# A cross-attention and FFN kernel: another prologue, the order of two small products, and where VectorE's spare work is put

## The chip, the cores and the metric

The kernel runs on one core of a Trainium2 chip. The metric is the device time of one execution in microseconds (us); the figure for a kernel is the median of its runs. One more execution was recorded by the profiler, and its rows are what the text below reads. The engines are TensorE (PE in the rows; PEld is its weight load), VectorE (DVE), ScalarE (ACT), GpSimd (POOL) and SyncE (SP, which here only issues transfers).

## What is computed

Sixteen samples `x` of 256 channels by 512 positions, all fp32. A layer norm over the positions, cross attention over channels-as-heads, a residual, another layer norm, and a feed-forward part whose weights are gathered from a table of 16 values:

```python
q = Wq @ norm(x) + bq; k = Wk @ ctx + bk; v = Wv @ ctx + bv      # per sample, 256x512
dot = einsum('bhdt,bhds->bhts', q, k) / sqrt(16)                 # 16 heads of 16 channels
mask = target_mask[..., :, None] * source_mask[..., None, :]
amap = softmax(mask * dot - (1 - mask) * 1e6, axis=-1) * mask
x = x + einsum('bhts,bhds->bhdt', amap, v)
n = norm(x)                                                     # rows of 512
gate, up = n @ lut[gate_idx].T, n @ lut[up_idx].T                # 512 -> 1376
x = x + (silu(gate) * up) @ lut[down_idx].T                      # 1376 -> 512
```

## The kernel before

The whole program is scheduled by hand: the order in which the Python code records instructions is the order on each engine.

**Attention.** `NK = 32` pairs of a sample and a channel half (k), each split into two units (u = 2k + e) of four heads, each unit into `NCH = 4` steps of 128 positions: 256 steps. Step s calls `scores(s + 7, s)`. For step s + 7 it makes the scores once (`pa`, L487) and VectorE reduces them to negated maxima (L503); for step s it makes the turned scores (`pb`, L495), which ScalarE exponentiates (L507). A padding row of the operands carries the maxima: `turn_max(u)` turns them by a small product (`pmx`, L512), VectorE copies them (`mx`, L514), and a transfer issued by POOL writes them into row 17 of each head of `qps` (L515). Another padding row carries the mask. `apply_v` (L529) multiplies with the values, `project` and `project_v` (both through L413) make q, k and v for later pairs. `pmx`, `pb`, and all of these projections share one pool of four PSUM buffers (`ps_b`).

Between the steps stand two dictionaries: `lumps[s]` holds PE work to be recorded in step s behind its scores, `after[s]` the rest. In 60 of the 64 units `turn_max` and a `project_v` fall into the same step, and before, `turn_max` is recorded first.

**The prologue.** Steps -7 to -1 only make scores and maxima. Ahead of them the first pair's tiles are made by `first_tile` (weights padded to the layout with gaps by `pad`, bias and mask added by VectorE at L371): the first unit's tiles ahead of step -7, the second unit's in steps -5 and -4. `warm` transposes the identity to keep PE at work while transfers land. `mbk` and `mb0` are the first sample's mask on all partitions, loaded with a broadcast; two small transfers patch rows of `mbk` (L380, L381).

**Lookups.** The gathered weights are built by VectorE from bit planes of the indices (`look_up`, L146 to L161). They are slotted between attention steps by a budget in ns:

```python
credit += 1930 + lasting[s] - taken[s] - (2590 if sa is not None else -500)
credit = min(credit, 1500.0)
while credit > 0:
    ns, op = next(queue, (0, None)); op(); credit -= ns
```

At step 229 (`turns - 3`) whatever is left of the `early` queue is recorded at once, and the first load of the `late` queue (`idx_r`) is issued.

**The FFN.** `gate_up(0..3, 0)`, then 84 units (p, o) of seven products each, a Strassen-like scheme: p is a pair of blocks of 512 columns, o a slice of 128 of the 1376 rows. The combined weights come from `combine_w` (L830), the combined inputs from `combine_x` (L839 to L842). The rest of the lookups and `combine_w` form one queue, `todo`; `fill(ns)` adds ns to a budget (capped at 3000) and records operations until it is spent. Units with p < 2 and o of 5 or 8 need weights that `todo` makes, so ahead of them the queue is drawn until they are recorded (`while o not in ready`). `turn_blocks` puts norm, turning and `combine_x` of later blocks into hooks of the units. Each unit calls its three hooks at three places.

Of the kernel before, what the change touches and what calls it, by code (L numbers as in the profile page):

```python
# [19 lines left out]
def kernel(  # L20
# [34 lines left out]
    nc = tc.nc  # L55
# [163 lines left out]
    with ExitStack() as att:  # L219
# [29 lines left out]
        def times(row, n):  # L249
            return row.rearrange("p (o t) -> p o t", o=1).to_broadcast([1, n, T])  # L250
# [45 lines left out]
        xn0 = p2.tile([P, NCC, T], F32, tag="xn", name="xn_0")  # L296
        mb0 = p2.tile([P, T], F32, tag="mb", name="mb_0")
        inp[0] = (cx0, xn0, mb0)
        for o in range(NCC):
            nc.sync.dma_start(xn0[:, o, :], x[0, o * P : (o + 1) * P, :])  # L300
        nc.scalar.dma_start(wk, wkT.rearrange("(o p) n -> p o n", p=P))
        nc.scalar.dma_start(cx0, src[0].rearrange("(o p) t -> p o t", p=P))
        nc.sync.dma_start(mk16, mask[:, 0, :])
        nc.sync.dma_start(mb0, mask[0, 0].partition_broadcast(P))

        w0 = pp.tile([P, 4, NCC, P], F32, tag="pt", name="w0")
        nc.gpsimd.memset(w0, 0.0)
        nc.gpsimd.memset(ones, 1.0)


        brow = pp.tile([P, P], F32, tag="pt", name="brow")
        nc.vector.memset(brow, 0.0)
        nc.vector.memset(brow[0:64, 16:P:32], NEG / QK)
        for i in range(2):
            nc.vector.memset(brow[64:P, 16 + i : P : 32], 1.0)

        mbk = pp.tile([P, T], F32, tag="pt", name="mbk")
        nc.sync.dma_start(mbk, mask[0, 0].partition_broadcast(P))
        nc.sync.dma_start(wq, wqT.rearrange("(o p) n -> p o n", p=P))
        for i, w in enumerate((bq, bk)):  # L320
            for e in range(2):
                at = 64 * i + 32 * e
                nc.gpsimd.dma_start(
                    brow[at : at + 1].rearrange("o (j e d) -> o j e d", e=2, d=D)[:, :, 0],
                    w[0:P].rearrange("(o j e d) -> o j e d", o=1, e=2, d=D)[:, :, e],
                )
# [6 lines left out]
        nc.scalar.dma_start(wv, wvT.rearrange("(o p) n -> p o n", p=P))  # L333
        nc.scalar.dma_start(bvb, bv.partition_broadcast(P))
        nc.scalar.dma_start(lut_b, lut.partition_broadcast(P))
        zeros = rpool.tile([P, T], F32, tag="rb", name="zeros", bufs=1)
        nc.gpsimd.memset(zeros, 0.0)

        def fill_rows():
            for i in (1, 0):  # L340
# [11 lines left out]
        def pad(i, e):  # L352
            w = (wk, wq)[i]
            to = w0[:, 2 * i + e].rearrange("p o (j r) -> p o j r", r=32)[:, :, :, 0:16]
            of = w[:, :, 0:P].rearrange("p o (j e d) -> p o j e d", e=2, d=D)[:, :, :, e]
            if i == 0:
                nc.vector.tensor_copy(to, of)
            else:
                nc.vector.tensor_scalar(to, of, QK, None, ALU.mult)

        def first_tile(which, e):
# [22 lines left out]
        pad(0, 0)  # L384
        rstd1_of(0, 1)
        norm1(0, nc.vector)
        pad(1, 0)
        pc = ps_b.tile([P, 512], F32, tag="b", name="pbrow")
        nc.tensor.transpose(pc[:, :P], brow, ident)
# [3 lines left out]
        first_tile("k", 0)  # L393
        first_tile("q", 0)
# [199 lines left out]

        lumps[-7].append(lambda: project(1, "k"))
        lumps[-6].append(lambda: project(1, "q"))
        after[-7].append(lambda: (pad(0, 1), pad(1, 1)))
        lumps[-5].append(lambda: first_tile("k", 1))
        lumps[-4].append(lambda: first_tile("q", 1))
# [66 lines left out]
        after[-4].append(lambda: set_ones(1))  # L666
# [85 lines left out]
        for s in range(min(min(after), min(lumps)), NSTEP + 2):  # L752
            sa = s + AHEAD if 0 <= s + AHEAD < NSTEP else None
            sb = s if 0 <= s < NSTEP else None
            if sa is not None or sb is not None:
                scores(sa, sb)
            for fn in lumps.pop(s, ()):
                fn()
            for fn in after.pop(s, ()):
                fn()  # L760
            if s >= 0:
                if s == turns - 3:
                    for _, op in early:
                        op()
                    load_rest()
                queue = early if s < turns - 3 else late
                credit += 1930 + lasting[s] - taken[s] - (2590 if sa is not None else -500)
                credit = min(credit, 1500.0)
                if s == NSTEP - 6:
                    closing.append(s)  # L770
                while credit > 0:
                    ns, op = next(queue, (0, None))
                    if op is None:
                        break
                    op()
                    credit -= ns
# [18 lines left out]
    with ExitStack() as ffn:  # L795
# [181 lines left out]
        def turn_blocks(n, at):  # L977

            k = 4 * n

            def step(i):
                if i:
                    turn2(k + i - 1)
                if i < 8:
                    norm2(k + i)
                    room[0] -= 550
                if i + 3 < 8:
                    load_x2(k + i + 3)
                if i == 8:
                    for _ in combine_x(n // 2):  # L990
                        room[0] -= 1230

            for i in range(3):
                hooks[at - 1, 2].append(lambda i=i: load_x2(k + i))
            for i in range(9):
                hooks[at + i // 3, i % 3].append(lambda i=i: step(i))
# [240 lines left out]
```

## Time and profile before

| what | us |
|---|---|
| median of 3 runs | 1821.81 (1821.67 to 1823.17) |
| profiled execution, its time | 1821.44 |
| profiled execution, its span | 1819.7 |
| TensorE busy | 1796.0 (99%) |
| VectorE busy | 1459.0 (80%) |
| ScalarE busy | 799.5 (44%) |
| GpSimd busy | 491.5 (27%) |
| first product of step -7 | 16.50 |
| first product of step 0 | 40.78 |

In the rows, the first number is the start from the beginning of the span, the second the duration, then engine, line, operation, output<-inputs, shape, and count; in brackets the idle time of that engine ahead of it and what ended it. In rows for a stretch each engine has its busy time and count, then the clock that TensorE was granted (1.00 is full), the share of the transfer engines in use, and GB/s.

### The profile page before, as it was taken

Reading aid. Unit: us, or ns where it says so; the run is one execution under the profiler, and the core shown is the slowest. Engines: PE = TensorE matmul, PEld = TensorE weight load, DVE = VectorE, ACT = ScalarE, POOL = GpSimd, SP = SyncE. Lnnn points to the kernel's source line nnn. Section 1 sums busy time; section 2 is a strip of 40 time slices with the busy share of each in tenths; the row PEclk is TensorE's granted clock in tenths of the full one; section 3 lists DMA queues with packets and bytes.
Section 4 is the critical chain, followed back from the end, with each engine's and each line's share of the span. In section 5 each row is a group of like instructions: output and inputs, shape, how many; then the busy total and the mean of one; then the engine's idle time right before and its main releaser. Section 6 shows DMA issues by size and latency. Waiting matters only on the chain.

```text
span 1819.7 us, 28550 instructions
## 1 busy us (share of the span) xinstructions
PE 1796.0 (99%) x10914; PEld 812.4 (45%) x10914; DVE 1459.0 (80%) x2030; ACT 799.5 (44%) x1523; POOL 491.5 (27%) x467
## 2 busy tenths in 40 slices
PE   8999999999999999999999999999999999999999
PEld 4333333333333333333234444444444444588887
DVE  6898988889898889898886799998888995353352
ACT  1777777777777777777676111112121111000000
POOL 4333343434333433433322122222222222000000
PEclk9999999999999999999999999999999999999999
DMA  6445534333433344444242211223231311533541
GB/s 187 129 143 149 149 115 129 121 114 96 127 114 125 92 128 137 148 121 141 87 120 75 69 58 55 74 81 106 68 104 42 116 51 44 182 132 126 176 132 58
DMA packets 118825, 201.07 MB, mean 111 GB/s; under 512 B 21781, under 2 KB 23961, under 8 KB 118689
## 3 DMA queue, kind: packets, MB, share of 16 engines
q1 hardware_dynamic: 114416, 196.21, 34.1%
q0 software_dynamic: 3168, 1.86, 0.5%
q8 instruction: 86, 1.41, 0.3%
q10 hardware_dynamic: 1104, 1.19, 0.2%
q14 instruction: 51, 0.41, 0.1%
HBM read 135.83 MB, written 58.10 MB: 107 GB/s over the span
## 4 chain that ended last, share of the span: by engine, by line
PE 92%; DVE 4%; DMA 1%; issue 0%; ACT 0%; SPq 0%; POOL 0%; ACTq 0%; DVEq 0%; POOLq 0%
PE p L934 27%; PE pa L487 15%; PE pv L529 12%; PE pb L495 11%; PE q L1140 11%; PE pv L413 3%; PE pq L413 3%; PE pk L413 3%; PE po L1121 2%; DVE nm L503 2%; PE q L1145 1%; PE pgu L914 1%; PE pmx L512 1%; PE pt L215 1%; DMA x2t<-x 1%; DVE chosen L161 0%
## 5 line engine op out<-in xcount | busy, mean ns | idle before, releaser
L503 DVE TENSOR_REDUCE nm<-pa 128x2 f32<-128x1024 f32 x512 | 603.3, 1220 | 103.8 <-PE pb L495 97.5
L507 ACT ACTIVATE pt<-pb 128x512 f32<-128x512 f32 x1024 | 530.0, 603 | 108.8 <-PE pb L495 107.7
L487 PE MATMUL pa<-kp,qp 32*128 32x512 f32 x2048 | 515.0, 616 | 9.5 <-DVE nm L503 6.9
L495 PE MATMUL pb<-qp,kp 32*128 32x512 f32 x2048 | 514.9, 617 | 0.0
L487 PEld LDWEIGHTS pa<-kp,qp 32*128 32x128 f32 x2048 | 179.5, 184 | 208.7 <-DVE nm L503 163.1
L529 PE MATMUL pv<-pt,va 128*32 128x512 f32 x2048 | 246.2, 598 | 0.0
L495 PEld LDWEIGHTS pb<-qp,kp 32*128 32x128 f32 x2048 | 203.4, 183 | 83.5 <-issue 52.4
L934 PE MATMUL p<-xe,wu 128*128 128x512 f32 (+1 forms) x336 | 158.1, 593 | 1.0 <-DVE w L938 1.0
L934 PE MATMUL p<-xT,sw 128*128 128x512 f32 (+1 forms) x336 | 157.9, 592 | 0.0
L934 PE MATMUL p<-xT,wg 128*128 128x512 f32 (+1 forms) x336 | 157.9, 592 | 0.0
L961 POOL TENSOR_TENSOR ha<-ha,sg 128x512 f32<-128x512 f32 (+1 forms) x42 | 60.4, 1438 | 344.3 <-DVE ha L938 326.0
L966 ACT ACTIVATE w<-w 128x512 f32<-128x512 f32 (+1 forms) x42 | 26.5, 630 | 241.4 <-DVE w L938 241.4
L529 PEld LDWEIGHTS pv<-pt,va 128*32 128x32 f32 x2048 | 53.4, 109 | 173.1 <-ACT pt L507 97.1
L515 POOL DMA_DIRECT2D qp<-mx x64 | 37.8, 591 | 313.1 <-DVE mx L514 290.4
L1156 ACT COPY q<-q 128x256 f32<-128x256 f32 x14 | 5.2, 372 | 254.4 <-PE q L1140 254.4
L534 ACT COPY us<-pv 128x512 f32<-128x512 f32 x128 | 74.9, 585 | 91.7 <-PE pv L529 91.0
L934 PEld LDWEIGHTS p<-xe,wu 128*128 128x128 f32 (+1 forms) x336 | 62.8, 187 | 83.0 <-issue 71.3
L934 PEld LDWEIGHTS p<-xT,wg 128*128 128x128 f32 (+1 forms) x336 | 62.7, 187 | 79.2 <-issue 75.4
L934 PEld LDWEIGHTS p<-xT,sw 128*128 128x128 f32 (+1 forms) x336 | 62.1, 187 | 75.4 <-issue 73.9
L948 ACT ACTIVATE sg<-sg 128x512 f32<-128x512 f32 (+1 forms) x42 | 26.5, 631 | 152.4 <-DVE sg L938 152.4
L541 POOL TENSOR_TENSOR us<-us,us 128x512 f32<-128x512 f32 x64 | 82.3, 1286 | 16.5 <-ACT us L534 16.5
L429 POOL TENSOR_TENSOR natk<-natk,mb 128x512 f32<-128x512 f32 x31 | 40.0, 1289 | 157.7 <-ACT natk L426 152.0
(205 smaller groups left out, 2375.1 us busy)
## 6 DMA issues: line engine op xcount, KB each, us to landing
x2t<-x SPq DMA_DIRECT2D x96, 256.0 KB
h<-h SPq DMA_DIRECT2D x7, 2560.0 KB
kp<-kd SPq DMA_DIRECT2D x62, 256.0 KB
qp<-qd SPq DMA_DIRECT2D x62, 256.0 KB
h<-ha SPq DMA_DIRECT2D x38, 256.0 KB
h<-hb SPq DMA_DIRECT2D x38, 256.0 KB
rb<-rd SPq DMA_DIRECT2D x32, 256.0 KB
xr<-in_x_dram SPq DMA_DIRECT2D x32, 256.0 KB
```

The lines of the kernel that those rows point to most:

```text
L413: nc.tensor.matmul(ps[32 * j : 32 * j + 32], weights(o, slice(first + 32 * j, first + 32 * j + 32)), moving(o), start=(o == 0), stop=(o == ...
L429: nc.gpsimd.tensor_tensor(t, t, mb, ALU.mult)
L487: nc.tensor.matmul(pa[:, jj, :], qps[ua % 4][at, ca * P : (ca + 1) * P], kps[ua % 4][at, :], start=True, stop=True,)
L495: nc.tensor.matmul(pb, kps[ub % 4][at, cb * P : (cb + 1) * P], qps[ub % 4][at, :], start=True, stop=True,)
L503: nc.vector.tensor_reduce(nms[ua][:, 2 * half : 2 * half + 2, ca], pa, AX.X, ALU.max, negate=True)
L507: nc.scalar.activation(pts[sb][:, j, :], pb, AF.Exp)
L529: nc.tensor.matmul(ps[32 * j : 32 * j + 32, :], va[:, at : at + 32], pt[:, j, :], start=(i == 0), stop=(i == 1),)
L534: nc.scalar.copy(us[u, half], ps)
L541: nc.gpsimd.tensor_tensor(a, a, b, ALU.add)
L934: nc.tensor.matmul(ps, a[:, h, at], b[:, h, :], start=h == 0, stop=h == 1)
L961: nc.gpsimd.tensor_tensor(ha, ha, sg, ALU.mult)
L1140: nc.tensor.matmul(ps, a[:, o, first_t], b[:, o, :], start=o == 0, stop=o == HO - 1 and not more,)
```

## The change

Six edits:

1. The prologue. VectorE's clearing of small tiles and the tiny transfers come first: two copies of the first mask row into `msrc`, and the bias entries into `brow`, the latter now issued by ScalarE's queue instead of POOL's. All large loads go to SP. `mbk` and `mb0` are no longer loaded with a broadcast; a product with a selection matrix `sel` spreads the mask rows (`pm`) and ScalarE copies the result. The warm-up has 16 and 24 transposes instead of 60. ScalarE does the padding for the second unit. All four first tiles are made ahead of step -7. `project(2, "k")` and `(2, "q")` move from steps -1 and 0 to -2 and -1; the first `project_v` go from steps -3 to -1 to steps -5 and -4; the loads of wv, bv and the table move to SP behind step -8; the filling of padding rows and the next loads from behind step -8 to behind -7.
2. `turn_max` is recorded behind `project_v` where both are in one step.
3. The credit is charged 2565 instead of 2590 ns per step.
4. `turn_blocks` starts one hook earlier.
5. `fill(6500)` is new ahead of `gate_up(0, 0)`; `fill(6000)` and `fill(3000)` around `gate_up(3, 0)` become one `fill(2500)`.
6. `combine_x(1)` is recorded operation by operation in hooks of the first unit (one in each of the first two, two in the third), each with `fill(-1230)`.

```diff
+        msrc = xpool.tile([P, T], F32, tag="xT", name="msrc")
+        sel = xpool.tile([P, 2, P], F32, tag="xT", name="sel")
+        nc.vector.memset(msrc, 0.0)
+        nc.vector.memset(brow, 0.0)
+        for i in range(2):
+            nc.sync.dma_start(msrc[32 * i : 32 * i + 1], mask[0, 0:1, :])
...
+                nc.scalar.dma_start(
+                    brow[at : at + 1].rearrange("o (j e d) -> o j e d", e=2, d=D)[:, :, 0],
...
-        nc.scalar.dma_start(wk, wkT.rearrange("(o p) n -> p o n", p=P))
-        nc.scalar.dma_start(cx0, src[0].rearrange("(o p) t -> p o t", p=P))
+        nc.sync.dma_start(wk, wkT.rearrange("(o p) n -> p o n", p=P))
+        nc.sync.dma_start(cx0, src[0].rearrange("(o p) t -> p o t", p=P))
+        nc.sync.dma_start(wq, wqT.rearrange("(o p) n -> p o n", p=P))
         nc.sync.dma_start(mk16, mask[:, 0, :])
-        nc.sync.dma_start(mb0, mask[0, 0].partition_broadcast(P))
...
-        nc.sync.dma_start(mbk, mask[0, 0].partition_broadcast(P))
-        nc.sync.dma_start(wq, wqT.rearrange("(o p) n -> p o n", p=P))
...
+            for o in range(NCC):
+                if e:
+                    nc.scalar.activation(to[:, o], of[:, o], AF.Copy, scale=QK if i else 1.0)
...
-        warm(60)
-        nc.vector.tensor_scalar(mk16, mk16, -1.0, None, ALU.add)
-        nc.sync.dma_start(mbk[16:P:32, :], times(mk16[0:1], 4))
-        nc.sync.dma_start(mbk[17:P:32, :], ones[0:4])
+        warm(16)
+        nc.vector.tensor_scalar(msrc[32:33], msrc[32:33], -1.0, None, ALU.add)
+        pm = ps_a.tile([P, 2, 512], F32, tag="a", name="pm")
+        for i, to in enumerate((mbk, mb0)):
+            nc.tensor.matmul(pm[:, i, :], sel[0:96, i, :], msrc[0:96], start=True, stop=True)
+            nc.scalar.copy(to, pm[:, i, :])
+        pc = ps_b.tile([P, 512], F32, tag="b", name="pbrow")
+        nc.tensor.transpose(pc[:, :P], brow, ident)
+        warm(24)
...
+        pad(0, 1)
+        pad(1, 1)
+        for e in range(2):
+            first_tile("k", e)
+            first_tile("q", e)
...
-        lumps[-1].append(lambda: project(2, "k"))
-        lumps[0].append(lambda: project(2, "q"))
+        lumps[-2].append(lambda: project(2, "k"))
+        lumps[-1].append(lambda: project(2, "q"))
...
-        for u in range(NU):
-            lumps[4 * u - 3].append(lambda u=u: turn_max(u))
-        lumps[-3].append(lambda: project_v(0, 0))
-        lumps[-2] += [lambda: project_v(0, 1), lambda: project_v(1, 0)]
-        lumps[-1].append(lambda: project_v(1, 1))
+        lumps[-5] += [lambda: project_v(0, 0), lambda: project_v(0, 1)]
+        lumps[-4] += [lambda: project_v(1, 0), lambda: project_v(1, 1)]
...
                 lumps[8 * k - 15 + 4 * i].append(lambda k=k, i=i: project_v(k, i))
                 after[8 * k - 13 + 4 * i].append(lambda k=k, i=i: mask_v(k, i))
+        for u in range(NU):
+            lumps[4 * u - 3].append(lambda u=u: turn_max(u))
...
-        after[-8] += [fill_rows, lambda: (load_xs(2), load_xs(3), load_b(1), load_wide(0))]
+        after[-8].append(load_v)
+        after[-7] += [fill_rows, lambda: (load_xs(2), load_xs(3), load_b(1), load_wide(0))]
...
-                credit += 1930 + lasting[s] - taken[s] - (2590 if sa is not None else -500)
+                credit += 1930 + lasting[s] - taken[s] - (2565 if sa is not None else -500)
...
-        turn_blocks(4, order.index((1, 8)))
-        turn_blocks(6, order.index((2, 5)))
+        turn_blocks(4, 3 * order.index((1, 8)) - 1)
+        turn_blocks(6, 3 * order.index((2, 5)) - 1)
...
+        fill(6500)
         gate_up(0, 0)
...
-        fill(6000)
+        fill(2500)
         gate_up(3, 0)
-        for _ in combine_x(1):
-            pass
-        fill(3000)
+        second = combine_x(1)
+        for i in range(4):
+            hooks[0, min(i, 2)].append(lambda: (next(second, None), fill(-1230)))
```

More of the change, by code (lines that the diff above doesn't have):

```diff
@@ L298 @@
         inp[0] = (cx0, xn0, mb0)
+        msrc = xpool.tile([P, T], F32, tag="xT", name="msrc")
+        sel = xpool.tile([P, 2, P], F32, tag="xT", name="sel")
+        brow = pp.tile([P, P], F32, tag="pt", name="brow")
+        nc.vector.memset(msrc, 0.0)
+        nc.vector.memset(brow, 0.0)
+        for i in range(2):
+            nc.sync.dma_start(msrc[32 * i : 32 * i + 1], mask[0, 0:1, :])
+        nc.vector.memset(brow[0:64, 16:P:32], NEG / QK)
+        for i in range(2):
+            nc.vector.memset(brow[64:P, 16 + i : P : 32], 1.0)
+        for i, w in enumerate((bk, bq)):
+            for e in range(2):
+                at = 64 * (1 - i) + 32 * e
+                nc.scalar.dma_start(
+                    brow[at : at + 1].rearrange("o (j e d) -> o j e d", e=2, d=D)[:, :, 0],
+                    w[0:P].rearrange("(o j e d) -> o j e d", o=1, e=2, d=D)[:, :, e],
+                )
         for o in range(NCC):
             nc.sync.dma_start(xn0[:, o, :], x[0, o * P : (o + 1) * P, :])
-        nc.scalar.dma_start(wk, wkT.rearrange("(o p) n -> p o n", p=P))
-        nc.scalar.dma_start(cx0, src[0].rearrange("(o p) t -> p o t", p=P))
+        nc.sync.dma_start(wk, wkT.rearrange("(o p) n -> p o n", p=P))
+        nc.sync.dma_start(cx0, src[0].rearrange("(o p) t -> p o t", p=P))
+        nc.sync.dma_start(wq, wqT.rearrange("(o p) n -> p o n", p=P))
         nc.sync.dma_start(mk16, mask[:, 0, :])
-        nc.sync.dma_start(mb0, mask[0, 0].partition_broadcast(P))
+        nc.vector.memset(msrc[64:65], 1.0)
+        nc.vector.memset(sel, 0.0)
+        nc.vector.memset(sel[0:1], 1.0)
+        for i in range(2):
+            nc.vector.memset(sel[0:1, 0, 16 + i : P : 32], 0.0)
+            nc.vector.memset(sel[32 + 32 * i : 33 + 32 * i, 0, 16 + i : P : 32], 1.0)
         w0 = pp.tile([P, 4, NCC, P], F32, tag="pt", name="w0")
@@ L308 @@
         nc.gpsimd.memset(ones, 1.0)
[L311 to L315, printed above, removed]
-        mbk = pp.tile([P, T], F32, tag="pt", name="mbk")
-        nc.sync.dma_start(mbk, mask[0, 0].partition_broadcast(P))
-        nc.sync.dma_start(wq, wqT.rearrange("(o p) n -> p o n", p=P))
[L320 to L326, printed above, removed]
+        mbk = pp.tile([P, T], F32, tag="pt", name="mbk")
         n = B * NCH
@@ L332, with load_v @@
         nc.gpsimd.dma_start(mq16, mask[:, 0, :])
-        nc.scalar.dma_start(wv, wvT.rearrange("(o p) n -> p o n", p=P))
-        nc.scalar.dma_start(bvb, bv.partition_broadcast(P))
-        nc.scalar.dma_start(lut_b, lut.partition_broadcast(P))
         zeros = rpool.tile([P, T], F32, tag="rb", name="zeros", bufs=1)
         nc.gpsimd.memset(zeros, 0.0)
+        def load_v():
+            nc.sync.dma_start(wv, wvT.rearrange("(o p) n -> p o n", p=P))
+            nc.sync.dma_start(bvb, bv.partition_broadcast(P))
+            nc.sync.dma_start(lut_b, lut.partition_broadcast(P))
         def fill_rows():
@@ L355, in pad @@
             of = w[:, :, 0:P].rearrange("p o (j e d) -> p o j e d", e=2, d=D)[:, :, :, e]
-            if i == 0:
+            for o in range(NCC):
+                if e:
+                    nc.scalar.activation(to[:, o], of[:, o], AF.Copy, scale=QK if i else 1.0)
+            if not e and i == 0:
                 nc.vector.tensor_copy(to, of)
-            else:
+            elif not e:
                 nc.vector.tensor_scalar(to, of, QK, None, ALU.mult)
@@ L376, in warm @@
                 nc.tensor.transpose(ps[:, :P], ident, ident)
-        warm(60)
-        nc.vector.tensor_scalar(mk16, mk16, -1.0, None, ALU.add)
-        nc.sync.dma_start(mbk[16:P:32, :], times(mk16[0:1], 4))
-        nc.sync.dma_start(mbk[17:P:32, :], ones[0:4])
+        warm(16)
[7 more added lines that the diff above has]
+        warm(24)
         for o in range(NCC):
             row_stats(p2, mv1[:, o, :], xn0[:, o, :], f"a0_{o}")
[L384 to L389, printed above, removed]
         bcol = pp.tile([P, P], F32, tag="pt", name="bcol")
@@ L392 @@
         nc.vector.tensor_scalar(bcol[:, 0:64], pc[:, 0:64], QK, None, ALU.mult)
-        first_tile("k", 0)
-        first_tile("q", 0)
+        rstd1_of(0, 1)
+        pad(0, 0)
+        norm1(0, nc.vector)
+        pad(1, 0)
+        pad(0, 1)
+        pad(1, 1)
+        for e in range(2):
+            first_tile("k", e)
+            first_tile("q", e)
+        nc.vector.tensor_scalar(mk16, mk16, -1.0, None, ALU.add)
         pc = ps_b.tile([P, 512], F32, tag="b", name="pcols")
@@ L596 @@
         lumps[-6].append(lambda: project(1, "q"))
-        after[-7].append(lambda: (pad(0, 1), pad(1, 1)))
-        lumps[-5].append(lambda: first_tile("k", 1))
-        lumps[-4].append(lambda: first_tile("q", 1))
         after[-6].append(lambda: send(1, "k"))
@@ L663 @@
             spread_out(stats_at[NCC * hi - 1] + 1, rstd1_of(lo, hi, newton_rstd))
-        after[-8] += [fill_rows, lambda: (load_xs(2), load_xs(3), load_b(1), load_wide(0))]
+        after[-8].append(load_v)
+        after[-7] += [fill_rows, lambda: (load_xs(2), load_xs(3), load_b(1), load_wide(0))]
         after[-7].append(lambda: set_ones(0))
-        after[-4].append(lambda: set_ones(1))
+        after[-6].append(lambda: set_ones(1))
         after[-2].append(lambda: norm1(1, nc.gpsimd))
@@ L993, in turn_blocks @@
             for i in range(3):
-                hooks[at - 1, 2].append(lambda i=i: load_x2(k + i))
+                hooks[divmod(at - 1, 3)].append(lambda i=i: load_x2(k + i))
             for i in range(9):
-                hooks[at + i // 3, i % 3].append(lambda i=i: step(i))
-        turn_blocks(4, order.index((1, 8)))
-        turn_blocks(6, order.index((2, 5)))
+                hooks[divmod(at + i, 3)].append(lambda i=i: step(i))
+        turn_blocks(4, 3 * order.index((1, 8)) - 1)
+        turn_blocks(6, 3 * order.index((2, 5)))
         for i in range(8):
```

## The prediction

> **What bounds the kernel now.** I read the page first: busy shares, then the chain that ended last.
>
> ```profile
> span 1819.7 us, 28550 instructions
> PE 1796.0 (99%) x10914; PEld 812.4 (45%) x10914; DVE 1459.0 (80%) x2030; ACT 799.5 (44%) x1523; POOL 491.5 (27%) x467
> ...
> PE 92%; DVE 4%; DMA 1%; issue 0%; ACT 0%; SPq 0%; POOL 0%; ACTq 0%; DVEq 0%; POOLq 0%
> ```
>
> TensorE is busy for 99% and carries 92% of the chain. No arithmetic of weight leaves it here, so the change can only win or lose in the places where TensorE waits. The table by stretches finds them (busy time of PE, PEld, DVE, ACT, POOL, then clock, DMA share, GB/s):
>
> ```profile
> 10.00:20.00 10.00, 7.48 (x40) 2.73 (x38) 5.82 (x13) 0.44 (x1) 2.58 (x5) 1.00 0.89 271
> 40.00:50.00 10.00, 8.41 (x86) 3.23 (x82) 7.75 (x9) 8.81 (x17) 4.24 (x5) 1.00 0.29 67
> ...
> 200.00:400.00 200.00, 199.02 (x1758) 69.37 (x1754) 178.71 (x216) 147.08 (x286) 79.23 (x76) 1.00 0.38 117
> ...
> 897.00:903.00 6.00, 1.97 (x20) 0.34 (x12) 5.93 (x6) 0.78 (x2) 1.08 (x1) 1.00 0.17 50
> 903.00:907.00 4.00, 4.00 (x24) 1.01 (x24) 3.60 (x9) 2.17 (x4) 0.00 (x0) 0.57 0.13 29
> ...
> 1190.00:1206.00 16.00, 16.00 (x39) 7.13 (x38) 15.83 (x29) 1.76 (x4) 3.68 (x3) 1.00 0.18 66
> ```
>
> TensorE loses time in the prologue and at 897, where the granted clock then falls to 0.57. Between 1190 and 1206 it loses none, but VectorE is full (15.83 of 16). Last, the timeline at these places, and one project_v unit:
>
> ```profile
> 15.04 0.75 DVE L371 SCALAR_TENSOR_TENSOR kp<-pk_first,bcol,mbk 128x512 f32<-128x512 f32 x1 [2.29 <-DMA mbk<-mrows]
> ...
> 17.68 2.36 DVE L503 TENSOR_REDUCE nm<-pa 128x2 f32<-128x1024 f32 x2 [0.58 <-PE pa L487]
> ```
> ```profile
> 41.36 1.28 ACT L507 ACT_TABLE_LOAD   x1
> 42.65 2.07 ACT L507 ACTIVATE pt<-pb 128x512 f32<-128x512 f32 x4
> ...
> 402.78 2.06 ACT L507 ACTIVATE pt<-pb 128x512 f32<-128x512 f32 x4 [0.42 <-PE pb L495]
> ```
> ```profile
> 403.51 0.41 PE L512 MATMUL pmx<-ident,nm 128*32 128x128 f32 x2
> 403.92 1.07 PE L413 MATMUL pv<-wv,ctx 128*32 128x256 f32 x16
> ...
> 901.97 0.69 PE L487 MATMUL pa<-kp,qp 32*128 32x512 f32 x1 [4.03 <-DVE nm L503]
> ```
> ```profile
> 894.82 1.17 DVE L157 TENSOR_SCALAR chosen<-chosen,lut_x,lut_b 128x688 int32<-128x688 int32 x2
> 896.02 3.83 DVE L161 COPY_PREDICATED chosen<-chosen,chosen 128x688 int32<-128x688 int32 x2
> 899.88 0.92 DVE L161 COPY_PREDICATED wg<-idx,chosen 128x688 int32<-128x688 int32 x1
> 900.70 2.34 DVE L503 TENSOR_REDUCE nm<-pa 128x2 f32<-128x1024 f32 x2
> ```
>
> **Part by part.** The sums are against the profiled execution (1821.44 us), which lies 0.37 below the median of the runs shown.
>
> *Prologue, +2.0.* Before, the first pa starts at 16.50 and its reduction at 17.68, held by the mask patch of mbk (15.04). After, a longer chain replaces it: msrc lands (estimate 4.3: issued about 1.3, then 3.0, as x1 took, whose landing let mbk be issued at 4.18), one VectorE operation, product pm0 (0.9 at the half clock of the start), ScalarE copy 0.6, pm1, copy 0.6, and then a second ACT_TABLE_LOAD: Copy now runs before the square root, so the load at 5.10 no longer hides under the loads. 1.28 + 0.30 + VectorE's 0.33, pad 0.21, norm1 1.08 and pad 0.23 bring the first product tiles to about 11.2; wq, issued once a tiny transfer has landed, comes at much the same time. Four first tiles at 1.72 (such groups start 1.71 to 1.78 apart) end at 18.1, so pa is 1.6 later; VectorE still owes qp1 (0.75) and two 0.42 operations, so the first reduction is about 2.5 later. Later, the two first tiles of steps -5 and -4 are gone from PE (2 x 1.72 = -3.4). Project(2,q) moves from step 0 into step -1, where it meets norm1(1): statistics (1.5 after the reduction of step -2), root, two small operations and POOL's 1.51 end 4.0 after that reduction, while PE is free 1.1 after it: +2.9. Sum 2.5 - 3.4 + 2.9 = +2.0; SP's and ACT's queues issue earlier or idle. POOL's six fills of padding rows (3.7 of issuing) stand behind natk and still land before the fetch at step -2; load_v on SP comes before step -7. Bounds: 0, if the q wait overlaps what ScalarE's exp table load (1.28) holds up in step 0 anyway; +4.5, if msrc or wq lands late.
>
> Here a rule speaks against the change: the Trainium skill, "ScalarE: Activation LUTs", What ACT_TABLE_LOAD costs, puts a switch at 1283 ns of load and about 1380 ns of drain, 2.66 us. The row at 41.36 shows 1.28, with the exp at its heels at 42.65, and the copy ahead ended at 41.34: no drain. By the row the sum stays; by the page it is 1.4 worse. I take the row.
>
> *project_v ahead of turn_max, -4.2.* In 60 units PE runs pmx in 0.41 for about 0.2 of work, since project_v then waits for the PSUM buffer that the second exp frees. Swapped, project_v takes the first exp's buffer and pmx the second's: at most 0.2 x 60 = 12. But the step after needs the fourth exp's buffer for its last pb: exps end at 404.84, and the step could start only slightly before its 404.92. I take 0.07 x 60 = 4.2 and keep +1 to -12. The copy of the maxima follows the reductions (ended 405.19) as before; its transfer has three steps to land.
>
> *credit 2590 to 2565, -3.3.* 25 ns in each of 229 steps lets 5.7 us of lookups start earlier, so the five operations at 894.82-900.7 are done by step 225. In the built order only two operations of the late set remain in step 229, and the first waits for idx_r, issued at 893.48 and landing, by an estimate from its packets, at 898.5. The reductions then start near 899.2 instead of 900.70, PE idles about 2.7 instead of 4.03. Steps start at 893.63, 901.97 and 907.66 where such steps take 3.78: 4.56 and 1.91 are lost, of which 1.4 and 1.9 return. Bounds -6 (idx_r early) and -1. Steady steps have 1.0 or more of VectorE slack, which covers 25 ns; without that cover the price would be 5.7.
>
> *combine_x(1) spread over four hooks, -1.0.* Its 1.23 operations no longer run in one row ahead of the first unit's adds, where PE waited 0.70 to 0.96 at 1033.6.
>
> *fill budgets, +3.4.* fill(-1230) four times puts 4.9 us of VectorE work behind. In the built order nine operations (a TENSOR_SCALAR, three COPY_PREDICATED at 0.54, four combine operations at 0.88, one at 0.41: 6.1) now stand in one row ahead of the first add of unit (0,8), because that unit forces its weights. The longest pause in adds that PE passed without idling there is 2.6 (1193.37 to 1195.97), and 6.1 - 2.6 is about 3.4. VectorE, full in this stretch, gives no cover. Bounds +2.5 and +6.
>
> Here too a rule bears: "TensorE: Matmul & The Clock Gate", Part 1, says that an idle window of some 3.4 us halves the clock, and that a busy one of as much restores it. The row 903-907 agrees (4.03 idle, then 0.57). So credit's 2.7 saves the cold stretch too, while 3.4 at (0,8) is on the edge: by the rule at its strictest, +1.7 more, sum -1.5 instead of -3.2.
>
> *turn_blocks one slot earlier, -0.1.* PE waits 1.91 for xe (L841) at 1273.59; the same operations begin a product earlier but then hold up that product's adds (-1.5 to +0.5). Fewer warm-up products, fill(6500) (VectorE idles 9 us there, before ht at 1000.57) and the tail cost nothing: the first stands beside the loads.
>
> Sum: +2.0 - 4.2 - 3.3 - 1.0 + 3.4 - 0.1 = -3.2, so 1818.2 in the profiled execution and 1818.6 on the median; I say 1818.4.
>
> **Rivals.** *The swap frees its full 0.2*: for it, PE waits on just that exp in each unit; against it, the fourth exp's end. -11.0 in all: 1810.5, or 1808 if the stall at 230 goes whole. *The burst at (0,8) is covered* by products in hand: -6.6, 1815; against it, the full VectorE. *VectorE runs behind in the FFN*: slower. Two units, (0,5) and (0,8), force their weights, and the lookups ahead of both are put behind by the same 4.9 us. A stop that turns cold costs its 3.4 and some 1.7 of half clock (half of a 3.4 stretch; step 231 lost 1.91). (0,8) turned cold (+1.7) and a stop at (0,5) as well (+5.1) make -3.2 + 6.8 = +3.6; four long forms in the two rows (1.96 instead of 0.88, as one at 1194) bring it to +7.9: 1825.5 to 1829.7. It decides from the second stop on; for it, the 15.83 of 16; against it, before passes both units unstalled. *The change does not do what it says*: the swap frees nothing, because the fourth exp sets each step, and idx_r takes the place of the five lookups: +2.0 - 1.0 + 3.4 - 0.1 = +4.3, 1826.
>
> **How the numbers follow.** A measurement of this kernel tells about 0.2% (3.6 us) from no change. The sum as worked: 0.48 (its centre lies on that edge: 0.21 faster, 0.19 same, 0.08 slower). Full swap: 0.22, faster. Covered burst: 0.06, faster. VectorE behind: 0.14 (0.12 slower, 0.02 same). Not what it says: 0.10 (0.06 slower, 0.04 same). Together 0.49 faster, 0.25 same, 0.26 slower. The sum's own range is 1813 to 1824; the range given, 1810.5 to 1826.5, leaves out the far ends of the first and third rivals.
>
> **What would show it.** Right: first pa near 18, step 2 near 51.6; no row of five lookups at step 229 but a VectorE wait on idx_r, PE idle under 3.4 and clock 1.00 to 907; pmx after project_v in 0.2, steps of 3.3 by a few hundredths shorter; a PE wait of 2.5 to 6 before unit (0,8). Wrong: steady steps unchanged or 0.2 shorter, a first pa beyond 20, or new PE waits in several FFN units.

## The result

The changed kernel is slower: a median of 1828.82 us (13 runs, 1824.79 to 1831.19) against 1822.20 (13 runs, 1821.39 to 1827.38). The ratio is 1.0029, with a 95% interval of 1.0022 to 1.0037, some 5.3 us. The prediction said 1818.4, with a range of 1810.5 to 1826.5, and gave "slower" a chance of 0.26.

The page of the changed kernel, first lines and chain:

```profile
span 1826.7 us, 28516 instructions
PE 1800.9 (99%) x10898; PEld 840.9 (46%) x10898; DVE 1463.2 (80%) x2037; ACT 796.3 (44%) x1530; POOL 503.2 (28%) x463
...
PE 90%; DVE 4%; DMA 1%; issue 1%; ACT 0%; POOL 0%; SPq 0%; POOLq 0%; ACTq 0%; DVEq 0%
```

TensorE does fewer products than before (10898 against 10914) and is busy for 4.9 us longer. Busy time grows without work when the clock is low, which the stretches show (busy PE, PEld, DVE, ACT, POOL, then clock, DMA share, GB/s):

```profile
30.00:40.00 10.00, 9.02 (x70) 2.58 (x70) 8.12 (x11) 0.74 (x2) 3.24 (x5) 0.83 0.51 151
40.00:50.00 10.00, 7.44 (x47) 2.30 (x47) 5.63 (x7) 4.07 (x7) 4.04 (x4) 0.83 0.30 108
...
897.00:903.00 6.00, 5.31 (x54) 2.20 (x50) 2.09 (x3) 4.34 (x9) 2.54 (x3) 1.00 0.72 212
903.00:910.00 7.00, 5.01 (x28) 1.22 (x32) 6.72 (x12) 2.17 (x4) 0.00 (x0) 0.76 0.08 19
1190.00:1200.00 10.00, 7.53 (x18) 3.04 (x16) 9.56 (x16) 1.52 (x3) 2.72 (x2) 1.00 0.07 26
1200.00:1210.00 10.00, 7.90 (x13) 3.51 (x14) 6.92 (x13) 0.63 (x1) 0.00 (x0) 0.66 0.25 79
```

Three places have a clock below 1.00: the steps ahead of step 0, the stretch behind 903, and the one behind 1200. Before, only the second had one. The starts of the same products in both traces, subtracted, say what each place cost:

| where | before | after | lead of before, us |
|---|---|---|---|
| step -7, first pa | 16.50 | 18.00 | 1.50 |
| step 0 | 40.77 | 46.63 | 5.86 |
| step 2 | 49.62 | 54.15 | 4.53 |
| step 229 | 890.15 | 895.16 | 5.01 |
| step 231 | 901.97 | 904.99 | 3.02 |
| first unit of the FFN | 1025.00 | 1027.42 | 2.42 |
| second unit, (1,1) | 1037.98 | 1039.43 | 1.45 |
| unit (0,8) | 1194.20 | 1195.65 | 1.45 |
| half a unit later | 1200.20 | 1208.95 | 8.74 |
| unit (2,0) and the half behind it | 1269.80, 1277.98 | 1278.55, 1285.66 | 8.74, 7.68 |

So the prologue lost 4.5, all steps between 2 and 229 together 0.5, step 229 returned 2.0, the spread combine_x 1.0, unit (0,8) lost 7.3, and turn_blocks returned 1.1. The waits of before that stand behind the two gains in the FFN:

```profile
1034.44 1.98 PE L934 MATMUL p<-xe,wu 128*128 128x512 f32 x4 [0.70 <-DVE w L938]
...
1273.59 1.98 PE L934 MATMUL p<-xe,sw 128*128 128x512 f32 x4 [1.91 <-DVE xe L841]
```

In the changed kernel the first is gone, and the second is 0.84 (at 1281.26, for the add that writes hb). Of the two calls of turn_blocks only the first, for the blocks from 4 on, starts a hook earlier: the second reads `turn_blocks(6, 3 * order.index((2, 5)))` in the changed kernel, without the `- 1` of the diff above, and fills the hooks that it filled before.

The rows behind this, TensorE first. In the prologue, the projections of steps -2 and -1 take 3.5 and 3.6 instead of 1.92, and the second waits for norm1:

```profile
36.46 3.51 PE L434 MATMUL pk<-ctx,wk 128*32 128x512 f32 x16
39.91 1.14 PE L508 MATMUL pa<-kp,qp 32*128 32x512 f32 x8
43.09 3.61 PE L434 MATMUL pq<-xn,wq 128*32 128x512 f32 x16 [2.04 <-POOL xn L286]
```

Before, the same two, in steps -1 and 0:

```profile
38.06 1.92 PE L413 MATMUL pk<-ctx,wk 128*32 128x512 f32 x16
...
43.35 1.92 PE L413 MATMUL pq<-xn,wq 128*32 128x512 f32 x16 [0.57 <-POOL va L454]
```

At step 229, VectorE waits for the late indices, and TensorE for VectorE:

```profile
903.21 0.34 DVE L146 TENSOR_SCALAR late_xn<-idx_r 128x344 int32<-128x344 int32 x1 [4.12 <-DMA idx_r<-in_L_ffn_gate_idx_dram]
```
```profile
904.99 0.69 PE L508 MATMUL pa<-kp,qp 32*128 32x512 f32 x1 [2.68 <-DVE nm L524]
...
907.63 3.13 PE L434 MATMUL pk<-ctx,wk 128*32 128x512 f32 x16
```

At unit (0,8), the second product reads the combined weights `sw`. TensorE waits for them, and then takes 3.78 for what took 1.88 before; the first row is from the changed kernel, the second from before:

```profile
1202.10 3.78 PE L953 MATMUL p<-xe,sw 128*128 128x512 f32 x4 [4.57 <-DVE sw L849]
```
```profile
1195.91 1.88 PE L934 MATMUL p<-xe,sw 128*128 128x512 f32 x4
```

What VectorE did in the meantime, in the changed kernel; the second combine operation ends at 1202.04:

```profile
1198.15 1.46 DVE L161 COPY_PREDICATED tb_l<-b_l,tc_l 128x344 int32<-128x344 int32 x1
1199.65 0.54 DVE L161 COPY_PREDICATED wu<-idx_l,tb_l 128x344 int32<-128x344 int32 x1
1200.22 0.89 DVE L849 TENSOR_TENSOR sw<-wu 128x704 f32<-128x704 f32 x1
1201.15 0.89 DVE L849 TENSOR_TENSOR sw<-sw,wg 128x704 f32<-128x704 f32 x1
```

The 1.46 is a long form: the same operation on the same shape takes 0.54 in the next row. In the traces the long forms go with GpSimd. All 70 VectorE operations of the changed kernel that took over 0.3 us more than the median of their kind (same line, tiles and shape), and all 75 of before, overlap an operation on GpSimd; this one starts at 1198.15, under a GpSimd operation that runs from 1197.91 to 1199.21. Not every overlap makes one long (493 in the changed kernel did not), and no run here moves the GpSimd operation, so this is shown by the timing alone.

### The profile page after: what moved, and what is told of

It reads as the page before. It is cut to its first block, busy times and chain, and to the rows that moved or that the text cites. A ratio compares the mean times of both kernels' runs of the same rounds, so it can differ in the third digit from the quotient of the medians.

```text
span 1826.7 us, 28516 instructions
## 1 busy us (share of the span) xinstructions
PE 1800.9 (99%) x10898; PEld 840.9 (46%) x10898; DVE 1463.2 (80%) x2037; ACT 796.3 (44%) x1530; POOL 503.2 (28%) x463
## 4 chain that ended last, share of the span: by engine, by line
PE 90%; DVE 4%; DMA 1%; issue 1%; ACT 0%; POOL 0%; SPq 0%; POOLq 0%; ACTq 0%; DVEq 0%
PE p L953 27%; PE pa L508 15%; PE pv L550 12%; PE pb L516 11%; PE q L1160 11%; PE pq L434 3%; PE pk L434 3%; PE pv L434 3%; PE po L1141 2%; DVE nm L524 2%; PE q L1165 1%; PE pgu L933 1%; PE pt L215 1%; DMA x2t<-x 1%; PE pmx L533 1%
## 5 line engine op out<-in xcount | busy, mean ns | idle before, releaser
L508 PE MATMUL pa<-kp,qp 32*128 32x512 f32 x2048 | 524.5, 616 | 8.9 <-DVE nm L524 8.9
L508 PEld LDWEIGHTS pa<-kp,qp 32*128 32x128 f32 x2048 | 192.2, 184 | 201.9 <-DVE nm L524 162.8
L516 PEld LDWEIGHTS pb<-qp,kp 32*128 32x128 f32 x2048 | 220.9, 183 | 66.3 <-issue 41.0
L475 POOL TENSOR_TENSOR va<-vt,bvb 128x256 f32<-128x256 f32 x64 | 56.7, 887 | 242.5 <-ACT vt L474 224.9
```

The lines of the kernel that those rows point to most:

```text
L475: nc.gpsimd.tensor_tensor(vas[b % 2][:, c, :, 0:D], vt.rearrange("p (h d) -> p h d", d=D), bvb.rearrange("p (h d) -> p h d", d=D), ALU.add,)
L508: nc.tensor.matmul(pa[:, jj, :], qps[ua % 4][at, ca * P : (ca + 1) * P], kps[ua % 4][at, :], start=True, stop=True,)
L516: nc.tensor.matmul(pb, kps[ub % 4][at, cb * P : (cb + 1) * P], qps[ub % 4][at, :], start=True, stop=True,)
```

## When the clock falls

Every fall and rise of the clock in this trace lies on one grid of 3.413 us: half from 36.30 to 39.71, from 43.12 to 46.54, from 906.70 to 910.11 and from 1200.24 to 1207.07. (The 860.16 us from 46.54 to 906.70 are 252 times 3.4133, the 290.13 from 910.11 to 1200.24 are 85 times.) The windows of that grid, each with the one behind it:

```profile
32.89:36.30 3.41, 2.43 (x13) 0.68 (x10) 3.36 (x4) 0.00 (x0) 0.76 (x2) 1.00 0.37 118
36.30:39.71 3.41, 3.41 (x18) 0.59 (x16) 3.04 (x6) 0.00 (x0) 0.11 (x1) 0.50 0.64 179
39.71:43.12 3.41, 1.37 (x16) 0.35 (x13) 2.13 (x3) 0.87 (x2) 2.11 (x3) 1.00 0.41 153
43.12:46.54 3.42, 3.42 (x16) 0.58 (x16) 1.37 (x3) 0.00 (x0) 0.67 (x1) 0.50 0.42 143
903.29:906.70 3.41, 1.71 (x16) 0.62 (x16) 3.38 (x7) 0.51 (x2) 0.00 (x0) 1.00 0.01 2
906.70:910.11 3.41, 3.41 (x20) 0.59 (x16) 3.38 (x6) 1.66 (x4) 0.00 (x0) 0.50 0.19 44
1196.83:1200.24 3.41, 0.70 (x2) 0.00 (x0) 3.27 (x6) 1.10 (x2) 1.30 (x1) 1.00 0.26 97
1200.24:1203.65 3.41, 1.55 (x2) 0.83 (x3) 3.38 (x5) 0.00 (x0) 0.00 (x0) 0.50 0.68 211
```

A window with little TensorE work is followed by one at half clock. The busy time alone does not decide: 2.43 of 3.41 in the first row were too little, while 1.62 us of products on the whole array kept the clock before (from 1271.80 to 1275.21). The four products of a pa run side by side, each on a quarter of the array. I therefore weighed each product by the share of the array that it uses: 0.43 us for 512 columns of the whole array (the pace of the FFN's products), a quarter of that for a product on a quarter of it, three quarters for one on 96 of its 128 rows, spread evenly over its row's time. The first, third, fifth and seventh of these windows then hold 24, 29, 36 and 18% of a full window. In the fourteen profiles of this study, from the first record of the clock up to the last microseconds, all 34 windows at full clock with 36% or less were followed by half clock, and none with 37% or more (the lowest five: 37, 39, 39, 39, 40). Windows at half clock follow the same edge: behind 12 us, all six with 33% or less were followed by another at half clock, as in the last row above, and all 32 with 39% or more by full clock (ahead of 12 us one with 39%, in a_sqrt, was not). The edge itself is less sharp than that: with each product's work put at the start or at the end of its row's time instead, the two groups overlap by two points, between 35 and 39%.

This corrects how the prediction used the Trainium skill, "TensorE: Matmul & The Clock Gate", Part 1. The page says that the window is free-running; the prediction took its 3.4 us as the least length of one idle stretch, and so called 2.7 us safe. They were not: by the trace, what counts is the work in a fixed window, and 1.70 of the 2.68 us of that stall fell into one. The page also speaks of an idle window, where the windows here were up to 36% full; the measurement decides.

Where the grid lies differs from run to run, so the same stall can cost half a window in one run and nothing in the next. Two cases show it. The kernel before, b_swap and b_credit all have the wait of 1.91 at unit (2,0). The kernel before keeps its clock there; the other two run 3.41 us at half clock, from 1274.90 and from 1275.04, and in b_swap the two products behind the wait take 5.23 instead of 3.54. And a_fill (below), which has the prologue of the changed kernel, keeps its clock through it, with 37% in the thinnest window. In times: of 55 runs of the kernel before, timed beside a_fill, the six with a mean granted clock of 0.999 have a median of 1820.8 us, and the nine with 0.996 one of 1826.0. So a part of the scatter of the runs is the grid, and a single profile can be lucky or unlucky by some microseconds.

## The experiments

Each was timed over five rounds beside the kernel before on the same chip; 0.001 of a ratio is 1.8 us.

**One part of the change alone.** Four kernels, each the kernel before with one part:

```diff
 b_prologue: edits of the prologue, turn_max still ahead of project_v
 b_swap:
-        for u in range(NU):
-            lumps[4 * u - 3].append(lambda u=u: turn_max(u))
         ... (project_v)
+        for u in range(NU):
+            lumps[4 * u - 3].append(lambda u=u: turn_max(u))
 b_credit:  2590 -> 2565
 b_ffn:     turn_blocks, fill budgets, combine_x in hooks
```

> The kernel before with the new prologue alone. Theory: the prologue costs most of what was lost, because steps -3 to 0 leave TensorE with so little work in a fixed window of 3.41 us that its clock is halved twice: step 2 starts about 54 instead of 49.6, two half-clock stretches between 30 and 50, time +4 to +5 us, with a scatter of 2 us from how the windows fall. Rival: only the waits counted in the prediction, +2.0 us, clock full throughout.

> The kernel before with turn_max behind project_v alone. Theory: each of these steps is 0.21 shorter and the step behind it 0.21 longer, because the fourth exp sets when the next step's pb finds a buffer; sum of eight steps 29.36 as before, time within 1 us of before. Rivals: 0.07 us gained per unit, -4.2 us; or the full 0.2 us, -12 us.

> The kernel before with the credit charged 2565 instead of 2590 alone. Theory: the five lookups of step 229 are gone, VectorE waits some 4 us for idx_r instead, TensorE idles about 2.7 instead of 4.03 us; whether its clock halves behind that depends on where a fixed 3.41 us window falls, so -1.5 us with and -3.5 without. Rival: the larger budget makes VectorE late in steady steps too and gives the gain back, 0 or slower.

> The kernel before with the three edits of the FFN alone (combine_x spread, fill budgets, turn_blocks one hook earlier). Theory: -1.0 at the first unit, +6 to +7.5 at unit (0,8), of which about 4.6 are idle time of TensorE and the rest two windows of half clock, -1.1 at unit (2,0): +4 to +5.5 us. Rival: the row of operations at (0,8) is only reached late because the attention part leaves more lookups over; then before's lookups keep it under 3 us, and the sum is +1 or less.

| kernel | ratio to before | 95% interval | us |
|---|---|---|---|
| b_prologue | 1.0021 | 1.0012 to 1.0030 | +3.8 |
| b_swap | 0.9999 | 0.9990 to 1.0008 | -0.2 |
| b_credit | 0.9987 | 0.9980 to 0.9994 | -2.4 |
| b_ffn | 1.0023 | 1.0013 to 1.0033 | +4.2 |
| sum of the four | | | +5.4 |
| the changed kernel | 1.0029 | 1.0022 to 1.0037 | +5.3 |

The parts add up, within intervals of some 1.3 to 1.8 us each. In b_prologue the stretch ahead of step 0 has the clock of the changed kernel, and the rival with a full clock falls:

```profile
30.00:50.00 20.00, 16.98 (x118) 4.91 (x114) 13.15 (x18) 3.42 (x7) 8.42 (x11) 0.83 0.48 153
```

b_swap shows where the gain of the swap went. One such step and the start of the next, TensorE and ScalarE:

```profile
406.75 1.07 PE L413 MATMUL pv<-wv,ctx 128*32 128x256 f32 x16
407.63 0.38 PE L512 MATMUL pmx<-ident,nm 128*32 128x128 f32 x2
407.94 0.69 PE L487 MATMUL pa<-kp,qp 32*128 32x512 f32 x1
...
408.14 0.69 PE L495 MATMUL pb<-qp,kp 32*128 32x512 f32 x1
```
```profile
406.02 2.06 ACT L507 ACTIVATE pt<-pb 128x512 f32<-128x512 f32 x4 [0.42 <-PE pb L495]
```

The step is 3.13 long instead of 3.34. The next one then comes up against the fourth exp (ended 408.08): its second pb starts at 408.14, 0.19 behind its first (before, 404.94 behind 404.93), and the step is 3.95 long instead of 3.78. The eight steps of a pair have eight median lengths, which add up to 29.30 against 29.38 before: of the 0.21 that each of the two units saves, 0.17 comes back in the next step. The 0.08 left would make 2.4 us in the whole; the runs show -0.2, with an interval of -1.8 to +1.5. The profile says where it goes: single steps are longer. Over steps 2 to 227, what steps take beyond the median of their kind is 11.0 us in b_swap and 6.5 before; 1.9 of it is one step at half clock, from 264.56 on, where before has no fall. In the changed kernel the second of the two lengthened steps takes 4.03, and the eight medians make 29.37, so there the gain is gone already in the steady steps. By these rows the release of the last exp's buffer sets the pace, and not the order on TensorE; no run here moves that exp.

b_ffn has the wait at unit (0,8) as the changed kernel has it (4.56 for the combine operation, at 1202.03), so the attention part has no share in it.

**Undoing or mending one part of the changed kernel.**

```diff
 a_fill:
-        fill(6500)
         gate_up(0, 0)
-        fill(2500)
+        fill(6000)
         gate_up(3, 0)
-            hooks[0, min(i, 2)].append(lambda: (next(second, None), fill(-1230)))
+            hooks[0, min(i, 2)].append(lambda: next(second, None))
+        fill(3000)
 a_warm08:
             nc.scalar.copy(p1, product(1, a11, b11))
+            if (p, o) == (0, 8):
+                warm(36)
 a_warmpro:
-        lumps[-2].append(lambda: project(2, "k"))
-        lumps[-1].append(lambda: project(2, "q"))
+        lumps[-2] += [lambda: warm(6), lambda: project(2, "k")]
+        lumps[-1] += [lambda: warm(16), lambda: project(2, "q")]
+        lumps[-3].append(lambda: warm(8))
 a_idx:
-                if s == turns - 3:
+                if s == turns - 6:
```

> The changed kernel with the fill budgets of before (6000 and 3000 around gate_up(3,0), no fill(6500), no fill(-1230)), combine_x(1) still spread over the hooks. Theory: the budgets alone made the stop at unit (0,8); it goes (unit at 6.0 instead of 13.3 us), and the time falls by 4.5 to 7 us against the changed kernel: 1822 to 1824, a ratio to before near 1.000. Rival: the spread combine_x takes the room that the lookups had, and a stop of over 2 us stays; 1826 or more.

> The changed kernel with 36 transposes of the identity put into TensorE's wait at unit (0,8), between its first two products; they compute nothing that is used. Theory: a window of 3.41 us with under some 40% of TensorE work is followed by one at half clock; filled, the clock stays, and the unit falls from 13.3 to about 10.6 us: the wait of 4.6 stays, 2.7 go. Time some 1.5 to 2.7 us below the changed kernel. Rival: the clock is not set by TensorE's own work there; then nothing changes or the transposes cost up to 3.9 us.

> The changed kernel with 8, 6 and 16 transposes of the identity put into steps -3, -2 and -1 (behind turn_max, ahead of project(2,k) and ahead of project(2,q)); they compute nothing that is used. Theory: the two half-clock stretches between 36 and 47 go, projections there take 1.9 instead of 3.5 us, and step 2 starts at about 51.5 instead of 54.2: 2 to 3 us. Rival: VectorE's reductions and norm1 set the pace there whatever the clock; then step 2 stays within 0.5 us of 54.2.

> The changed kernel with the first load of the late lookups issued three steps earlier (end of step 226 instead of 229), the order on VectorE unchanged. Theory: VectorE's wait of 4.1 us for idx_r goes, TensorE's stall of 2.7 us ahead of step 231 and the half clock behind it with it: 3.5 to 4.6 us below the changed kernel. Rival: the next late load or a reduction is then late instead; under 1.5 us.

| kernel | ratio to before | 95% interval | against the changed kernel's 1.0029, us |
|---|---|---|---|
| a_fill | 0.9998 | 0.9991 to 1.0005 | -5.6 |
| a_warm08 | 1.0022 | 1.0012 to 1.0031 | -1.3 |
| a_warmpro | 1.0019 | 1.0012 to 1.0025 | -1.8 |
| a_idx | 1.0008 | 0.9999 to 1.0016 | -3.8 |

a_fill: the budgets alone made the stop. With those of before, unit (0,8) takes 6.01 to its half, as before, and its second product starts at 1197.04, right behind the first (1195.32).

a_warm08 parts the idle time from the clock. The transposes fill the wait, and the product behind them takes 1.96 instead of 3.78:

```profile
1196.88 4.38 PE L390 MATMUL warm<-ident 128*128 128x128 f32 x36
1201.72 1.96 PE L953 MATMUL p<-xe,sw 128*128 128x512 f32 x4 [0.47 <-DVE sw L849]
```

From (0,8) to its half are now 10.9 instead of 13.3 us: of the 7.3 us lost, about 2.4 were the clock's and 4.9 the wait's. The interval of the runs overlaps that of the changed kernel, so the time alone would not show it.

a_warmpro does the same for the prologue. Both projections run at full clock, though the wait for norm1 is as long as before:

```profile
37.27 1.92 PE L434 MATMUL pk<-ctx,wk 128*32 128x512 f32 x16
...
40.20 1.97 PE L390 MATMUL warm<-ident 128*128 128x128 f32 x16
42.30 1.92 PE L434 MATMUL pq<-xn,wq 128*32 128x512 f32 x16
```

Step 2 starts at 51.67, 2.5 earlier than in the changed kernel. The other 2.05 of its 4.53 are real waits and work, with the transposes' own time among them. Here too the intervals of the runs overlap, so the gain is read from the profile.

A lucky grid could have kept the clock in these two profiles. To exclude it, a window of 3.41 us was moved over the weighed work in small steps: wherever it lies, it holds 46% or more in a_warmpro between 28 and 54, and 77% or more in a_warm08 between 1193 and 1208. In the changed kernel the thinnest such windows hold 19 and 0%. So it was the transposes that kept the clock.

a_idx (what is left of the early lookups is recorded three steps earlier too): three steps of notice take VectorE's wait away, TensorE's stall of 2.68 becomes 0.42, and the projection behind it takes 1.92:

```profile
904.33 0.69 PE L508 MATMUL pa<-kp,qp 32*128 32x512 f32 x1 [0.42 <-DVE nm L524]
...
906.53 1.92 PE L434 MATMUL pk<-ctx,wk 128*32 128x512 f32 x16
```

**Two edits of the prologue that settled less.**

```diff
 a_sqrt: row_stats, rstd1_of(0, 1), pad(0, 0), norm1(0), pad(1, 0)
         ahead of the loop over pm and its nc.scalar.copy
 a_back:
-        lumps[-2].append(lambda: project(2, "k"))
-        lumps[-1].append(lambda: project(2, "q"))
+        lumps[-1].append(lambda: project(2, "k"))
+        lumps[0].append(lambda: project(2, "q"))
-        lumps[-5] += [lambda: project_v(0, 0), lambda: project_v(0, 1)]
-        lumps[-4] += [lambda: project_v(1, 0), lambda: project_v(1, 1)]
+        lumps[-3].append(lambda: project_v(0, 0))
+        lumps[-2] += [lambda: project_v(0, 1), lambda: project_v(1, 0)]
+        lumps[-1].append(lambda: project_v(1, 1))
```

> The changed kernel with the square root of the first sample's norm (and VectorE's work that follows from it) ahead of ScalarE's two copies of the mask product, so that one table load serves both. Theory: the second table load of 1.28 us and the copies ahead of it hold back the first tiles; without them the first tile starts near 9 instead of 10.9 and the first pa near 16 instead of 18; about 1.5 us of it reach step 2 and the end. Rival: wq or the context arrive no earlier than 10.5, then pa stays at 17.5 or later and the time does not change.

> The changed kernel with the first four project_v back in steps -3 to -1 and project(2,k), project(2,q) back in steps -1 and 0. Theory: moving them left steps -3 to -1 with under 36% of TensorE work in two windows; back, no window there falls under that, no half clock between 33 and 47, no wait of 2 us for norm1, and step 2 starts near 51.5 instead of 54.2, as with the filler: 1.5 to 3 us less. Rival: the work that comes back lengthens these steps by as much as the half clock did; within 0.5 us.

a_sqrt: ratio 1.0033 (1.0023 to 1.0042), no better than the changed kernel. One table load is gone, but the pad of wq waits for its transfer, and my edit put the bias columns behind it. The pool of four PSUM buffers holds the transposes of the warm-up until these columns are read, so 17 of them run behind 11.19, at half clock, and the first pa starts at 21.87 instead of 18.00:

```profile
10.61 0.23 DVE L373 TENSOR_SCALAR w<-wq 128x128 f32<-128x128 f32 x1 [1.67 <-DMA wq<-in_L_xattn_Wq_dram]
```
```profile
11.19 3.82 PE L390 MATMUL warm<-ident 128*128 128x128 f32 x17 [0.40 <-DVE bcol L409]
```

In the changed kernel that pad started at 11.63, so the second table load can have held it up by about 1.0 us and no more; whether it did was not settled.

a_back: ratio 1.0018 (1.0008 to 1.0027), about 2 us better, but the interval overlaps that of the changed kernel. In its profile half clock comes still, from 32.52 on, since with the first tiles gone from steps -5 and -4 these steps are now the empty ones (28% in the window ahead of it). Moving the small work back moves the hole; it does not fill it. It does take away the wait for norm1: from the first pa to step 2 pass 34.4 us instead of 36.2. That gain is hidden in the profile, since the warm-up fell to half clock from 8.62 and the first pa starts at 19.92 instead of 18.00.

**The mends together.** best1 is the kernel before with the credit of 2565, the first late load three steps earlier, combine_x in the hooks and turn_blocks one hook earlier; a_fixed is the changed kernel with the edits of a_fill, a_idx and a_warmpro.

> The kernel before (its prologue, its order of turn_max and project_v, its fill budgets) with the credit of 2565, the first late load three steps earlier, combine_x spread and turn_blocks one hook earlier. Theory: -2.4 of the credit, some -3.8 of the early load, -1 at units (0,1) to (2,0): -6 to -8 us against before, ratio 0.9955 to 0.9968, the fastest of all. Rival: the gain of the early load was already in the credit's run of before; -3 to -4, ratio 0.998.

> The changed kernel with the three mends together: the fill budgets of before, the first late load three steps earlier, and 30 transposes of the identity in steps -3 to -1 (which compute nothing that is used). Theory: the three causes are separate and add up: -5.6 - 3.8 - 1.8 us as the single runs gave them, a ratio to before of 0.997, and what then separates it from the fastest kernel of the last runs (0.9952) is the new prologue's own 2 us of waits and work. Rival: the stops share windows of the clock or slack on VectorE, so that mending one hides another; then the ratio stays at 0.999 or above.

best1: 1815.16 us (5 runs), ratio 0.9952 (0.9938 to 0.9966). a_fixed: 1814.79 us (5 runs), ratio 0.9959 (0.9945 to 0.9973). Both beat both kernels. In both profiles no window of the 1800 us behind the start is at half clock. In best1 this does not hang on the grid: the thinnest 3.41 us between 12 and 1800 hold 40%. In a_fixed one place could still fall (35% at 262.5, a thin place that b_swap has too). best1's page and its wait-free step 229:

```profile
span 1813.9 us, 28547 instructions
...
PE 1795.9 (99%) x10914; PEld 813.0 (45%) x10914; DVE 1459.2 (80%) x2030; ACT 799.7 (44%) x1523; POOL 494.6 (27%) x467
```
```profile
895.64 0.32 DVE L146 TENSOR_SCALAR late_xn<-idx_r 128x344 int32<-128x344 int32 x1
```

The mends of a_fixed brought at least their sum (0.9959 against the 0.997 expected, which the interval holds). The two versions cannot be told apart by these runs: in the profiles a_fixed starts step 2 at 52.07 and best1 at 50.33, while their spans are 1813.0 and 1813.9. So what the new prologue costs in the end, once the clock is kept, stays open; the expectation of 2 us is not confirmed.

## Why the prediction was wrong

Four terms of the sum were off, all to the same side: the swap, the wait at unit (0,8), the prologue and the credit. Two of them share one cause: the prediction counted idle stretches and not the work in a window of the clock.

*Prologue, +2.0 predicted; +4.5 in the profile, +3.8 in runs of it alone.* The chain was right: first pa predicted at 18.1, found at 18.00; first reduction +2.5, found +2.3 (19.95 against 17.68); the wait of project(2,q) 2.9, found 2.04. No drain follows the second table load, so it was right to take the row against the page: the copy ended at 8.66, the load ran from 8.68 to 9.96, the root started at 9.97. What failed is a cost put at nothing: the clock. The sum credited 3.4 us for the first tiles gone from steps -5 and -4 and moved project_v forward into these steps, and never asked what is left in steps -3 to -1. There the reductions of 2.36 set the pace, TensorE's work fell to 24 and 29% of a window, and two windows ran at half speed, 2.5 us by a_warmpro. With the clock kept, step 2 is 2.05 later, just the +2.0 of the forecast; that the sum fits so well is in part luck, since its term for the wait was 0.9 too large.

*Swap, -4.2 predicted; -0.2 (-1.8 to +1.5).* The prediction named the limit, the fourth exp, and then still took 0.07 a unit, the gap between the exps' end (404.84) and the step (404.92). It sized this on one step and did not look at the one behind: starting earlier moves the wait into the next step's second pb, which leaves 0.04 a unit in b_swap, lost again in single steps, and nothing in the changed kernel. The rival that the swap frees nothing was right in this (it also put the credit at nothing, which was wrong), and the one with the full 0.2 fell.

*Credit, -3.3 predicted; -2.0 in the profile, -2.4 in runs.* VectorE's wait, its cause and TensorE's 2.7 us (found 2.68) were right. What failed is the 1.9 us of half clock that it counted as saved, because the idle stretch was shorter than 3.4: the window of the clock held 36% of work, which was too little, and the 1.9 were lost again.

*Fill budgets, +3.4 predicted; +7.3 in the profile, about +5.6 by a_fill.* The place, the row of nine operations and the forced unit were right. What failed is the step from the row to the wait. The prediction took the whole row of 6.1 and subtracted the longest pause in adds that TensorE had passed (2.6). By the trace TensorE did not wait for the add behind the row: the unit's own second product waits for `sw`, which the sixth operation of the row completes, and so TensorE stood still for 4.57 (4.9 lost by a_warm08). Of this, 0.9 is the one long form in the row. The half clock, priced at 1.7 for the case that the stop turned cold, took 2.4. The rival "VectorE runs behind" had a cold stop, but its second one at (0,5) did not come, so it was right in its first term only.

*combine_x, -1.0; found -0.97. turn_blocks, -0.1; found -1.06*, inside its bounds: the operations began early enough to take a good half of the 1.91 away, and what is left is a wait for an add, the price that the prediction had named. No run has one of these two alone.

In sum, by the profile: 4.7 for the swap (all steps between 2 and 229 cost +0.5 instead of -4.2), 1.3 behind step 229, 2.5 in the prologue and 3.9 at (0,8), less 1.0 for turn_blocks: 11.4 us, of which the stretches between step 231 and the FFN and behind unit (2,0) gave back 0.6 each. The gap between the forecast of 1818.2 for the profiled execution and its 1828.53 is 10.3.

## What to carry to other kernels

Before removing or delaying work around a stall, add up what TensorE still does in any 3.4 us there: in these profiles 36% of a full window or less meant that the next one ran at half speed, however short each single wait was. Where a pipeline is paced by the last of several buffer releases, a swap that frees the first ones mostly moves the wait; sum a whole period, not the step. A load whose first reader is close behind its issue is cheap to move: three steps of notice brought 3.8 us, more than any other edit of the changed kernel but the undoing of its fill budgets. And when several profiles of one kernel differ, look first at where the clock fell.

## What the runs showed of the hardware that was not expected

- The clock's window lies on a grid of 3.413 us that is fixed within a run, and the work in it counts by how much of the array it uses: 34 of 34 windows with 36% or less were followed by half clock, none with 37% or more.
- Useless work kept the clock: 30 transposes ahead of step 0 and 36 at one unit took away 2.5 and 2.4 us in the profiles.
- VectorE's long forms (1.46 instead of 0.54, and the like) all lie under an operation on GpSimd: 70 of 70 in the changed kernel, 75 of 75 before.
- A load of 172 KB took 4.7 us from its issue at 898.49 to its reader at 903.21, where 212 GB/s were moving.
